# First layer of a four-layer network: gathers of the middle taps in three parts a round, finished tiles a round later

## The chip, the core and the metric

The kernel is written in Bass and Tile for one NeuronCore of a Trainium2 chip. The core has five engines that run side by side, each in its own program order: TensorE (PE, matrix products into PSUM), VectorE (DVE), ScalarE (ACT), GpSimd (POOL), and SyncE (SP), which only issues DMAs here. They wait for one another by semaphores. The metric is the device time of one execution in microseconds; smaller is better.

## The reference, cut to the first layer

The network has four layers over an input of 4 images, 128 channels, 64 x 64 places. Only the first is touched by the change: a group norm, then a deformable convolution with 8 groups and 9 taps, a product with `w_out`, a batch norm, and x * sigmoid(x), added to the input.

```python
val = xf @ w_value + b_value                     # xf: normed input, places x channels
om  = (xf @ w_off + b_off).reshape(N, P, G, OM)  # per place and group: 18 offsets, 9 masks
sy, sx = base_y + offset[..., 1], base_x + offset[..., 0]
...
for dy, dx, wgt in ((0, 0, (1 - ty) * (1 - tx)), (0, 1, (1 - ty) * tx),
                    (1, 0, ty * (1 - tx)), (1, 1, ty * tx)):
    acc = acc + gather(iy, ix) * (wgt * valid(iy, ix))[..., None]
out = (acc * mask[..., None]).sum(axis=3)
out = out.reshape(N, P, C) @ w_out + b_out
...
return out * jax.nn.sigmoid(out)                 # after the batch norm
```

The later layers (a convolution with a state-space scan, a cosine "attention" with a feed-forward part, tanh attention, and two expert mixtures) run after it, unchanged.

## The kernel before

**Two ways for a place.** Nearly all offsets are small. A place whose offsets stay within R = 1 is computed without any gather: a 5 x 5 window of values around it (W = 5) is multiplied with 25 weights per group. Places with a larger offset, up to R2 = 2, are "exceptions": each image may have up to 128 of them, one to a partition, and they are computed from a 7 x 7 window (W2 = 7) whose rows are gathered one by one from a table in DRAM.

**Tiles and rounds.** An image is 8 tiles (NQS = 8) of TG = 4 columns of 128 places. The loop at the end of the first layer runs over rounds r; round r does tile r of the 32 tiles of the 4 images (so rounds 0 to 7 are image 0, 8 to 15 image 1, and so on), and beside it

- projects a tile of the next image (`project`, `evict`: values to the table `tab`, offsets to `oms`) and ranks its exceptions (`flags`, `rank`, `collect`),
- makes the weights of tile r + 1 (`tents`, `weights`),
- takes one step of the generator `exceptions(n)` after each of the five parts k = 0 to 4 of the round,
- turns tile r - 1 (`cast`, then `turn`: four transposes and a copy into `aT`), and
- finishes tiles whose image has its exceptions ready.

In part k, PE adds the products of window column k into PSUM (`accumulate`, five 512-wide products with the identity), and DVE makes those of column k + 1 (`multiply`, tile `pr`, 128 x 2560). `multiply` also has SP load that column for the next tile (`move`, tile `v`). In part 4 the first product of the next round is made, ahead of the step of `exceptions`.

**The exceptions.** `exceptions(n)` starts in the second round of image n (r % 8 == 1). It makes the row numbers `idx`, and then for each of the seven columns s gathers seven sets of rows into `px` (seven indirect DMAs of POOL, one for each u) with two `px` buffers. The weights of the exceptions are worked out after the first gather. Then, for each s, column s + 1 is gathered and column s is multiplied with its weights on DVE and added into `total`. In the end PE folds `total` (`pe1`), multiplies with `w_out` (`pe2`), and ACT leaves the result in `tw` (`mended[n]`). Each `yield` ends a step. A gather has a `yield` inside it, after its fourth DMA, so its seven DMAs fall into steps of four and three, and the generator has 17 steps: the gathers lie in steps 1 to 14, the last product in step 15, `pe1` in 16, `pe2` in 17. Step 17 is taken in part 1 of the fourth round after the start's (r % 8 == 4).

**Finishing.** `spread` transposes the marks of the exceptions of a tile (`ohs`, made by DVE in part 0, into `oT`), and `finish`, one part later, multiplies the turned tile `aT` with `w_out` and adds the exceptions through `oT` and `tw`; ACT applies the batch norm and the last function, and POOL adds the result into X (`settle`). It needs `mended[n]`. The dictionary `ends` says in which round which tiles are finished; a finish starts in part 2, a second one follows in part 3 (or 4). `turned` holds the copies `aT` until then, in 4 buffers.

**What sets the order.** All engines' instructions in this loop go through `InOrder`, which keeps each engine in the program's order; only the DMAs of SP are free of it. A DVE product that waits for gathered rows therefore holds up everything behind it on DVE. PSUM tiles of `turn`, `spread`, `finish` and the exceptions share two buffers (tag `pt`).

In the profile nearly all instructions of this loop are put down to line 82, the helper that keeps the order, so they are told apart by the names of their tiles.

Of the kernel before, what the change touches and what calls it, by code (L numbers as in the profile page):

```python
# [8 lines left out]
F32 = mybir.dt.float32  # L9
# [7 lines left out]
P = 128  # L17
# [71 lines left out]
class Kernel:  # L89
# [33 lines left out]
    def layer0(self):  # L123
# [12 lines left out]
        TG = 4  # L136
# [6 lines left out]
        with ExitStack() as outer:  # L143
            fp = outer.enter_context(tc.tile_pool(name="d0x", bufs=1))
            over = fp.tile([1, 1], I32, name="over")
            with ExitStack() as ctx:
# [4 lines left out]
                qp = ctx.enter_context(tc.tile_pool(name="d0q", bufs=2))  # L151
# [7 lines left out]
                for n in range(NB):  # L159
                    for h in range(2):  # L160
                        s = slice(n * L + h * L // 2, n * L + (h + 1) * L // 2)
# [139 lines left out]
                def tents(om, m, r):  # L301

                    D = 2 * r + 1
                    o = om[:, 0:18 * m]
                    tent = wp.tile([P, D, 18 * m], F32, name=f"tent{r}", tag="tent")
                    ab = wp.tile([P, 18 * m], F32, name=f"ab{r}", tag="t0")
                    for d in range(-r, r + 1):
                        if abs(d) == r:
                            k = R2 + r - 1
                            nc.scalar.activation(tent[:, d + r, :], o, AF.Relu, bias=shift[:, k:k + 1],  # L310
                                                 scale=float(d // r))
                        else:
                            nc.scalar.activation(ab, o, AF.Abs, bias=shift[:, d + R2:d + R2 + 1])
                            nc.scalar.activation(tent[:, d + r, :], ab, AF.Relu, bias=self.ones[:, 0:1],
                                                 scale=-1.0)
                    return tent
# [131 lines left out]


                mended = {}  # L450

                def exceptions(n):
                    oc = wp.tile([P, NO + 1, G], F32, name="oc")
                    ocf = oc.rearrange("p j g -> p (j g)")
                    nc.scalar.copy(ocf, rare[n][:, 0:(NO + 1) * G])
                    idx = wp.tile([P, W2, W2], I32, name="idx")
                    nc.vector.tensor_scalar(idx, reach, oc[:, NO, 0:1], None, ALU.add)
                    flat = tabs[n].rearrange("x y c -> (x y) c")
                    wt = wp.tile([P, W2, W2, G], F32, name="wt2")

                    def gather(s):
                        px = qp.tile([P, W2, P], F32, name="px")
                        for u in range(W2):
                            nc.gpsimd.indirect_dma_start(
                                out=px[:, u, :], out_offset=None, in_=flat,
                                in_offset=bass.IndirectOffsetOnAxis(ap=idx[:, s, u:u + 1], axis=0))
                            if u == 3:
                                yield
                        return px

                    px = yield from gather(0)
                    yield "weights"
                    for _ in weights(ocf, tents(ocf, G, R2), wt, G, R2):
                        pass
                    total = wp.tile([P, W2, P], F32, name="total")
                    for s in range(W2):
                        after = (yield from gather(s + 1)) if s + 1 < W2 else None
                        dst = px if s else total
                        nc.vector.tensor_tensor(
                            dst.rearrange("p u (g c) -> p (u g) c", c=CG),  # L480
                            px.rearrange("p u (g c) -> p (u g) c", c=CG),
                            wt[:, s].rearrange("p u g -> p (u g)").unsqueeze(2).to_broadcast([P, W2 * G, CG]),
                            ALU.mult)
                        if s:
                            nc.vector.tensor_tensor(total, total, px, ALU.add)
                        px = after
                        yield
                    ps = pt.tile([P, TG * P], F32, name="pe1", tag="pt")
                    for u in range(W2):
                        nc.tensor.matmul(ps[:, 0:P], total[:, u, :], self.ident, start=(u == 0), stop=(u == W2 - 1))  # L490
                    eT = sm.tile([P, P], F32, name="eT", bufs=1)
                    nc.scalar.copy(eT, ps[:, 0:P])
                    yield
                    ps = pt.tile([P, TG * P], F32, name="pe2", tag="pt")
                    nc.tensor.matmul(ps[:, 0:P], eT, w_out, start=True, stop=True)
                    tw = sm.tile([P, P], F32, name="tw", bufs=2)
                    nc.scalar.copy(tw, ps[:, 0:P])
                    mended[n] = tw
# [51 lines left out]
                def turn(i, at_):  # L550
                    pT = pt.tile([P, TG * P], F32, name="pT", tag="pt")
                    for k in range(TG):
                        nc.tensor.transpose(pT[:, k * P:(k + 1) * P], at_[:, k * P:(k + 1) * P], self.ident)
                    aT = qp.tile([P, TG * P], F32, name="aT", bufs=4)
                    nc.scalar.copy(aT, pT)
                    turned[i] = aT

# [21 lines left out]
                LAST_R = NB * NQS  # L579
                ends = {}  # L580
                for n in range(NB):
                    for k, qs in ((4, (0, 1)), (5, (2, 3)), (6, (4,)), (7, (5,)), (8, (6, 7))):
                        ends.setdefault(n * NQS + k, []).extend(n * NQS + q for q in qs)
                extra, stat, tent, wgen = None, None, None, None
                order(0)
# [1 line left out]
                for r in range(-4, LAST_R + 1):  # L587
# [34 lines left out]
                    for k in range(W):  # L622
# [29 lines left out]
                        if k == 1:  # L652
                            if at_ is not None:
                                turn(r - 1, at_)
# [1841 lines left out]
```

## Time and profile before

| | us |
|---|---|
| Three timed runs | 5593.98, 5611.95, 5615.91 (median 5611.95) |
| The profiled execution, its own time | 5601.23 |
| Its span in the profile | 5599.5 |
| First `pr` product starts | 108.2 |
| Last tile is added into X | 1145 |

The span of the profile and the time of the same execution are 1.7 us apart, so sums made in the profile can be read as time. The first layer takes the first fifth of the span; the rest does not depend on the change except by starting earlier or later.

Busy time of the engines from the first `pr` product (108.2 us) to the last (1128.7 us), 1020.5 us in all:

| Engine | busy us |
|---|---|
| PE | 921.5 |
| DVE | 874.4 |
| POOL | 414.9 |
| ACT | 231.2 |

Averages over this stretch hide that the rounds differ. Rounds that hold gathers have POOL busy most of their length; other rounds have POOL nearly idle. Some rows for the instructions that the change moves:

| Instruction | count | duration, us |
|---|---|---|
| gather `px<-tab,idx` (POOL) | 196 | 0.94 to 3.56, median 1.17 |
| product `px<-px,wt` (DVE) | 24 | 1.09 |
| sum `total<-total,px` (DVE) | 24 | 1.09 |
| product `pr<-v,wt` (DVE) | 160 | 2.82 |
| copy `aT<-pT` (ACT) | 32 | 0.59 |

A gather's duration is what POOL spends on it; the rows arrive after it. A row of the timeline has the start, the duration, the engine, the source line, the operation, the tiles (out<-in), the shape, and in brackets the idle time of the engine before it with what ended it.

### The profile page before, as it was taken

To read this page: it belongs to the slowest core of one execution; us is meant where nothing else is said; L and a number is where in the kernel's file an instruction comes from. 1 tells how busy PE (TensorE), PEld (TensorE's weight loads), DVE (VectorE), ACT (ScalarE), POOL (GpSimd) and SP (SyncE) were. 2 spreads that over 40 slices of the span, in tenths; PEclk is the share of its full clock that TensorE was granted. 3 is DMA by queue.
4 is the path that set the end of the run, shared out by engine and by line. 5 is a ranking of instruction groups with operands and counts; after the bars stand their busy time and mean duration, and the time that the engine had idled before them with its cause. 6 is when DMAs were issued, how large, how long until landed. Compare 5 with 4: busy or idle time off the path is not lost. (4 is left out here: it accounts for less than half of the span.)

```text
span 5599.5 us, 62830 instructions
## 1 busy us (share of the span) xinstructions
PE 4991.9 (89%) x21718; PEld 2404.9 (43%) x21718; DVE 4016.3 (72%) x7854; ACT 3113.9 (56%) x3785; POOL 3073.1 (55%) x3027
## 2 busy tenths in 40 slices
PE   6898989879999859999887899989998998999887
PEld 3454444335656523333443344434433444344443
DVE  6888988758876578786698565666566666665796
ACT  1122222146655345555431689878978987889431
POOL 0525253314444324454399577666766776667597
PEclk8999999989988779999899899999999999999899
DMA  5545454400000020000000000000000000000001
GB/s 171 126 131 128 124 132 127 98 6 1 16 16 12 27 61 1 1 1 1 6 31 16 16 1 1 1 1 1 1 1 1 1 1 1 1 1 1 5 1 61
DMA packets 66743, 185.21 MB, mean 33 GB/s; under 512 B 13158, under 2 KB 16038, under 8 KB 64744
## 3 DMA queue, kind: packets, MB, share of 16 engines
q1 hardware_dynamic: 55792, 163.68, 9.9%
q0 software_dynamic: 6272, 12.86, 1.4%
q10 hardware_dynamic: 4344, 4.50, 0.3%
q8 instruction: 175, 2.87, 0.2%
q14 instruction: 160, 1.31, 0.1%
HBM read 131.63 MB, written 49.36 MB: 32 GB/s over the span
## 5 line engine op out<-in xcount | busy, mean ns | idle before, releaser
L82 POOL TENSOR_TENSOR r<-r 128x512 f32<-128x512 f32 (+1 forms) x1088 | 1349.0, 1241 | 661.9 <-DVE r L82 597.0
L82 DVE TENSOR_TENSOR r<-r,num 128x1024 f32<-128x1024 f32 (+1 forms) x1088 | 970.4, 927 | 564.3 <-PE num L82 514.1
L82 PE MATMUL D<-F,G 32*128 32x512 f32 (+3 forms) x4608 | 1218.8, 589 | 1.9 <-POOL G L82 1.0
L82 PE MATMUL num<-F,G 32*128 32x512 f32 (+3 forms) x4608 | 1084.5, 604 | 105.4 <-DVE r L82 101.6
L82 ACT ACTIVATE r<-r 128x2048 f32<-128x2048 f32 (+4 forms) x610 | 1018.3, 1679 | 49.2 <-POOL r L82 3.4
L82 ACT ACTIVATE r<-D 128x1536 f32<-128x1536 f32 (+1 forms) x544 | 764.2, 1405 | 206.1 <-PE D L82 174.2
L82 PE MATMUL acc<-pr,ident 128*128 128x512 f32 x1600 | 749.4, 619 | 79.4 <-DVE pr L82 79.4
L82 PEld LDWEIGHTS D<-F,G 32*128 32x128 f32 x4608 | 507.2, 189 | 327.4 <-issue 217.2
L82 PE MATMUL acc<-r,v 128*128 128x512 f32 (+3 forms) x1152 | 606.4, 614 | 3.1 <-DVE aT L82 3.1
L82 PEld LDWEIGHTS num<-F,G 32*128 32x128 f32 x4608 | 394.4, 187 | 410.9 <-DVE r L82 239.5
L1886 PE MATMUL pex<-w_expert_w,vT 128*128 128x512 f32 x1024 | 489.5, 618 | 78.9 <-DVE x L1889 78.8
L1896 POOL TENSOR_TENSOR x<-x 128x512 f32<-128x512 f32 (+2 forms) x576 | 472.6, 820 | 103.3 <-DVE x L1889 73.3
L82 PEld LDWEIGHTS acc<-pr,ident 128*128 128x128 f32 x1600 | 309.9, 198 | 439.4 <-issue 340.2
L82 DVE TENSOR_TENSOR pr<-v,wt 128x2560 f32<-128x2560 f32 x160 | 452.7, 2835 | 30.3 <-PE acc L82 24.6
L82 PE MATMUL pff<-hid,w_ffn_w2T 128*128 128x512 f32 x1024 | 468.4, 600 | 0.0
L82 POOL DMA_INDIRECT px<-tab,idx x196 | 330.7, 1687 | 231.5 <-DVE idx L82 159.8
L82 POOL TENSOR_TENSOR X<-X,sl 128x512 f32<-128x512 f32 x32 | 87.9, 2746 | 491.5 <-ACT sl L82 491.5
L1889 DVE TENSOR_TENSOR x<-pex,gate 128x1024 f32<-128x1024 f32 x256 | 309.1, 1213 | 62.8 <-POOL X L1897 51.1
L82 PEld LDWEIGHTS acc<-r,v 128*128 128x128 f32 x1152 | 176.7, 190 | 393.1 <-issue 263.9
L1886 PEld LDWEIGHTS pex<-w_expert_w,vT 128*128 128x128 f32 x1024 | 184.0, 193 | 329.0 <-DVE x L1889 176.9
L82 ACT ACTIVATE hid<-phh,cols 128x512 f32<-128x512 f32 x320 | 198.9, 685 | 224.2 <-PE phh L82 224.2
L82 POOL TENSOR_TENSOR Y<-y,tm 128x64 f32<-128x64 f32 x256 | 115.9, 473 | 331.1 <-DVE w L82 164.3
(563 smaller groups left out, 7379.4 us busy)
## 6 DMA issues: line engine op xcount, KB each, us to landing
v<-tab SPq DMA_DIRECT2D x320, 256.0 KB
oms<-omw SPq DMA_DIRECT2D x32, 432.0 KB
omr<-oms SPq DMA_DIRECT2D x32, 432.0 KB
X<-in_x_dram SPq DMA_DIRECT2D x8, 1024.0 KB
tab<-vb SPq DMA_DIRECT2D x64, 128.0 KB
o<-o SPq DMA_DIRECT2D x32, 256.0 KB
oin<-o SPq DMA_DIRECT2D x32, 256.0 KB
kept<-X SPq DMA_DIRECT2D x4, 2048.0 KB
```

Of the source, the lines that this page charges most:

```text
L82: return lambda *args, **kwargs: self.tc.keep_in_program_order(op(*args, **kwargs))
L1886: nc.tensor.matmul(pex[:, 4 * h:4 * h + 4, :], vT[:, k, :], ew[:, 512 * h:512 * (h + 1)], start=True, stop=True)
L1889: nc.vector.tensor_tensor(x, pex, gate[:, k, :].unsqueeze(2).to_broadcast([P, NE, P]), ALU.mult)
L1896: nc.gpsimd.tensor_tensor(x[:, 0:w, :], x[:, 0:w, :], x[:, w:2 * w, :], ALU.add)
```

## The change

Three edits. First, the gathers of columns s = 1 to 5 (`PACED`) have their inner `yield` after the third and after the fifth DMA, so that seven DMAs fall into steps of three, two and two; columns 0 and 6 keep four and three. The generator then has 22 steps: gathers in steps 1 to 19, the products of columns 0 to 6 in steps 5, 8, 11, 14, 17, 19 and 20, `pe1` in step 21, `pe2` in step 22. Step 22 is taken in part 1 of the round with r % 8 == 5. Second, the tiles of an image are finished two a round, in the fifth to the eighth round counted from the image's first as 0, instead of 2, 2, 1, 1, 2 in the fourth to the eighth. Third, `aT` has five buffers.

```diff
                 mended = {}
+                PACED = range(1, 6)
 
                 def exceptions(n):
...
                             nc.gpsimd.indirect_dma_start(
                                 out=px[:, u, :], out_offset=None, in_=flat,
                                 in_offset=bass.IndirectOffsetOnAxis(ap=idx[:, s, u:u + 1], axis=0))
-                            if u == 3:
+                            if u == 3 and s not in PACED or u in (2, 4) and s in PACED:
                                 yield
                         return px
...
-                    aT = qp.tile([P, TG * P], F32, name="aT", bufs=4)
+                    aT = qp.tile([P, TG * P], F32, name="aT", bufs=5)
                     nc.scalar.copy(aT, pT)
                     turned[i] = aT
...
-                    for k, qs in ((4, (0, 1)), (5, (2, 3)), (6, (4,)), (7, (5,)), (8, (6, 7))):
+                    for k, qs in ((5, (0, 1)), (6, (2, 3)), (7, (4, 5)), (8, (6, 7))):
                         ends.setdefault(n * NQS + k, []).extend(n * NQS + q for q in qs)
```

## The prediction

> **What bounds the kernel now.** I read the granted clock and DMA rows of the page first, to place the first layer (it ends near 1145 us of 5599.5), then cut it into its rounds. A round starts at every fifth `pr` product on DVE. Image 1 spans rounds 9 to 16; this is the table of busy time by stretch over them. Columns: stretch, length, busy time and instructions of PE, PEld, DVE, ACT, POOL, then granted clock, DMA share, GB/s.
>
> ```profile
> 402.80:436.50 33.70, 29.15 (x78) 14.41 (x77) 31.16 (x50) 13.04 (x32) 22.53 (x13) 0.92 0.51 128
> 436.50:468.50 32.00, 28.57 (x78) 13.97 (x77) 29.40 (x41) 5.86 (x14) 27.62 (x15) 0.98 0.58 142
> 468.50:516.10 47.60, 34.74 (x92) 17.78 (x90) 38.17 (x60) 8.47 (x20) 34.45 (x23) 0.86 0.54 132
> 516.10:548.60 32.50, 29.36 (x90) 15.20 (x91) 28.52 (x47) 5.32 (x11) 1.27 (x1) 0.95 0.38 108
> 548.60:579.10 30.50, 30.50 (x91) 15.72 (x90) 26.77 (x46) 8.38 (x19) 7.32 (x2) 1.00 0.43 114
> 579.10:609.10 30.00, 30.00 (x87) 15.33 (x86) 25.94 (x41) 10.70 (x23) 6.55 (x2) 1.00 0.46 126
> 609.10:637.50 28.40, 28.40 (x84) 14.60 (x83) 25.79 (x42) 7.11 (x16) 2.85 (x1) 1.00 0.48 134
> 637.50:666.20 28.70, 28.70 (x87) 14.93 (x86) 26.44 (x45) 4.74 (x12) 3.64 (x1) 1.00 0.48 131
> ```
>
> Two regimes. Rounds 13 to 16 have PE busy from end to end: PE sets the time. In rounds 9 to 12, where the 49 gathers run on POOL, PE is below its length and DVE is the busiest, with a hole of 9.4 us in round 11. The waits of the first 1100 us say who made the hole (total, times, longest):
>
> ```profile
> POOL px L82 <- issue: 55.2, 181, 0.3
> DVE px L82 <- DMA px<-tab,idx: 46.5, 14, 7.3
> ```
>
> POOL stands 0.3 us between gathers 181 times out of 196: it issues without pause. DVE waits 46.5 us for gathered rows, and 3.6 us more in image 2 (put down to issue). The POOL and DVE timelines at the hole of round 11:
>
> ```profile
> 467.90 0.94 POOL L82 DMA_INDIRECT px<-tab,idx  x1 [0.30 <-issue]
> 469.15 2.99 POOL L82 DMA_INDIRECT px<-tab,idx  x1 [0.30 <-issue]
> 472.45 0.94 POOL L82 DMA_INDIRECT px<-tab,idx  x1 [0.31 <-issue]
> ```
>
> ```profile
> 468.50 2.83 DVE L82 TENSOR_TENSOR pr<-v,wt 128x2560 f32<-128x2560 f32 x1
> 476.22 1.10 DVE L82 TENSOR_TENSOR px<-px,wt 128x896 f32<-128x896 f32 x1 [4.89 <-DMA px<-tab,idx]
> ```
>
> The seventh gather of its tile ends on POOL at 472.1 and the product starts at 476.2: about 4 us of landing. DVE stands in program order, so every later product, and PE behind it, stands too. Image 3 is worst, because its rounds hold less DVE work while POOL's stay the same:
>
> ```profile
> 981.60:1023.30 41.70, 30.46 (x64) 12.96 (x64) 26.83 (x23) 6.20 (x15) 35.00 (x23) 0.88 0.56 120
> ```
>
> Why: before, a gather of 7 takes two of the five steps of a round, so 17.5 gathers a round. Start to start they are 2.02 us apart (mean over the four trains), 35.4 us a round against 25 to 31 us of DVE work. The px waits per image, from the waits of each four-round stretch: 6.2, 5.2, 13.9, 24.8, together 50.1 us.
>
> **Part 1, the three-part gathers.** Tiles 1 to 5 take three steps, so a round holds 11.7 gathers in the middle. Nothing is added: 196 gathers, 28 products, the same DMAs; no SP transfer moves. Steps per image go from 17 to 22. The products (1.09 + 1.09 us) shift: by the generator, the stretches of rounds 9 to 12 held products 0; 1, 2; 3, 4, 5; 6, and will hold none; 0, 1; 2, 3; 4, 5, with 6 at the start of round 13.
>
> What sets the new pace is the gather spacing under a busier DVE. Laying the POOL timeline against DVE's: the 35 intervals with DVE under half busy average 1.25 us, the 24 at 50 to 90% average 2.41, the 133 at 90% and more 2.16. So DVE work slows descriptor making already. A rule speaks against the change here: the Trainium skill, "SBUF — State Buffer", has a box on DVE blocking gathers of the POOL queue, and its section on the wrong bandwidth-pool intuition prices one at 0.62 us alone and 3.1 us beside a two-port DVE copy. At 3.1, a train is 49 x 3.1 = 152 us, longer than the four rounds before, and the change would lose. At 2.16 it is 106 us. I take the row: two thirds of today's intervals are already under a full DVE. The three steps between two products are some 18 us against 7 x 2.16 = 15.1, so POOL keeps up.
>
> One tight place stays: tile 6 can start only when product 4 frees its px buffer (two exist), and its product comes three steps later, as before. 7 x 2.16 + 3.5 landing is 18.6 against about 17.5 of DVE work: 1.1 us of wait per image; below nothing is excluded (a wait cannot be negative), above is 4.2 (spacing 2.6).
>
> DVE sums of the four rounds: today 127.1, 127.3, 121.4, 102.6 for images 0 to 3. Off come product 6 (2.17) and the marks of two tiles (eight `ohs`, 1.65): 3.8. Idle that stays is the length less DVE busy less the px waits, less the 3.7 and 3.6 us that DVE waited for PE in round 4 of images 0 and 1: 8.5, 9.7, 4.9, 8.7. To it I add 2.0 for the fourth round, now ruled by DVE and showing the waits of rounds 9 and 10 (1.2 for the rank and 0.8 for the accumulation), and the 1.1.
> - Image 0: 127.1 - 3.8 + 8.5 + 3.1 = 134.9, before 145.5: -10.6
> - Image 1: 127.3 - 3.8 + 9.7 + 3.1 = 136.3, before 145.8: -9.5
> - Image 2: 121.4 - 3.8 + 4.9 + 3.1 = 125.6, before 140.2: -14.6
> - Image 3: the same sum gives 110.6, but POOL is late: its train starts 12.0 us into the stretch, and 12.0 + 49 x 2.1 + 3.5, less the 2.8 of the `pr` ahead of product 6, is 115.6 (2.1 because DVE will be some 87% busy, between the train's 2.01 today and 2.16). Before 136.1: -20.5
>
> Sum -55.2 us. Below: 2.02 spacing gives image 3 back 4 us. Above: 2.41 costs 4 in image 2 and 15 in image 3.
>
> **Part 2, the finishes a round later.** Tiles 0 to 7 of an image are finished 2, 2, 2, 2 in rounds 5 to 8 where it was 2, 2, 1, 1, 2 in rounds 4 to 8. One finish on PE, from its timeline in round 13:
>
> ```profile
> 564.20 0.60 PE L82 MATMUL poh<-ident,ohs 128*128 128x128 f32 x4
> ...
> 569.50 1.02 PE L82 MATMUL pO<-aT,w_w_out 128*128 128x512 f32 x2
> 570.36 1.02 PE L82 MATMUL pO<-oT,tw 128*128 128x512 f32 x2
> 571.22 0.60 PE L82 MATMUL poh<-ident,ohs 128*128 128x128 f32 x4
> ```
>
> Start to start: 0.43 + 0.86 + 0.86 = 2.15 us. The turned tile's transposes start at 563.76, 594.24, 622.56, 650.89: 30.48 with two finishes, 28.32 with one, the same 2.16. These two finishes leave a round where DVE will rule and enter rounds 6 and 7, ruled by PE: +4.3. The sixteen short `pe` matmuls also move from round 4 to round 5, 0.108 each by the transposes' spacing: +1.7. So +6.0 per image, +24.1 in all; no cover hides it, since PE is 100% busy there (image 3's rounds 29 to 31 show DVE waiting 4.9 us a round for the accumulation, the same bound). PE may enter round 13 up to 2 us less behind, by the gap between `pr` and its accumulation today (1.8 to 2.2): I leave this as range.
>
> **Part 3, five buffers.** 2 KB a partition and no instruction. Tile 4's copy in round 5 precedes finish 0; the next reuse follows a finish by a round: no wait. Finishes wait for `tw` as now, one round later. On POOL the adds into X (1.3 to 3.9 us) come after the last gather in both orders; nobody queues behind them.
>
> A second rule: the Trainium skill, "TensorE: Matmul & The Clock Gate", on clock oscillation, says that idle gaps over some 3.4 us halve PE's clock. The row agrees in kind (PE's longest wait for `pr` is 4.5 us, clock 0.86 in round 11), and by the rule closing gaps would give round 11 up to 0.14 x 47.6 = 6.7 us of PE time. By the row that is worth nothing: round 10 has 0.98 and is still 32.0 us, with DVE at 29.4. I take 0.
>
> **Sum:** -55.2 + 24.1 = -31 us. Against the profiled run's own 5601.2 us: 5570. Against the median of 5612: 5581. The four known times average 5607, and I forecast 5575 between them. About 0.5% (28 us) is what a measurement can tell here, so the forecast stands close to that line.
>
> **Rivals.**
> - Gathers slow down to 2.4 us as DVE closes up. For it: the 2.41 of the middle class. Against: the fullest class has 2.16. It costs 19 us: -12, some 5595, within 0.5%.
> - POOL becomes the bound everywhere (slower). Stretches become train start (9.3, 11.3, 11.4, 12.0 us) + 49 s + 0.7. They lose all gain over the +24 at s = 2.53; at 3.1 the four are 87 us longer than today, and with +24 the time is about 5718. For it: the skill's price. Against: no class of intervals reaches 2.53.
> - The px waits are landing time, not rate, and stay. For it: products start 3 to 5 us after the last gather in nearly every tile. Against: tiles 4 and 5 of images 0 and 1, where round 3's statistics give POOL time, are used 12 us after, without a wait. Then 50 us stay, finishes and product moved: 5601 - 15 + 24 = 5610: no change.
>
> **Chances.** Forecast 0.62 (own range 5560 to 5592), slowed gathers 0.20, landing 0.09, POOL bound 0.09. Of the forecast's 0.62 some 0.08 falls short of 28 us; of the slowed gathers 0.03 is beyond it. Faster 0.57, same 0.34, slower 0.09. The range of 5555 to 5600 takes in the spacing's ends and the slowed gathers.
>
> **What will show it.** px waits under 10 us in all; rounds 9 to 12 near 32.5, 31, 41, 31.5; rounds 13 to 16 near 32, 30.5, 30.5, 30.5, PE full; image 3's four rounds near 115; gather spacing 2.1 to 2.2. Wrong if the spacing passes 2.4, if px waits stay over 25 us, or if rounds 13 to 16 grow by much more than 6 us together.

## The result, and the profile after

The changed kernel takes 5582.3 us (median of 17 runs, 5549.8 to 5592.8), the kernel before 5602.1 (median of 17 runs timed beside it). The ratio is 0.9962, with a 95% interval of 0.9951 to 0.9972: faster by 0.38%, some 21 us, where 31 had been forecast. In the profiled executions the last tile of the first layer is added into X at 1124.7 us where it was 1145.6, so the gain lies in the first layer.

Busy time by stretch, rounds 9 to 16 of the changed kernel (columns as before: stretch, length, PE, PEld, DVE, ACT, POOL, clock, DMA share, GB/s):

```profile
400.10:433.00 32.90, 28.35 (x77) 14.14 (x76) 30.35 (x48) 13.06 (x32) 21.92 (x13) 0.92 0.50 125
433.00:463.20 30.20, 28.84 (x79) 14.33 (x78) 28.25 (x41) 5.86 (x14) 23.12 (x13) 0.97 0.58 151
463.20:505.80 42.60, 32.58 (x92) 17.14 (x90) 36.04 (x59) 8.46 (x20) 24.30 (x17) 0.88 0.53 135
505.80:537.80 32.00, 27.77 (x69) 13.12 (x70) 29.01 (x41) 4.92 (x11) 16.41 (x9) 0.89 0.49 120
537.80:571.60 33.80, 29.64 (x97) 15.75 (x96) 28.62 (x48) 6.37 (x15) 6.54 (x2) 1.00 0.42 112
571.60:602.10 30.50, 30.50 (x92) 15.72 (x91) 26.77 (x46) 8.38 (x19) 7.32 (x2) 1.00 0.45 127
602.10:632.60 30.50, 30.50 (x92) 15.74 (x91) 26.77 (x46) 8.38 (x19) 7.32 (x2) 1.00 0.45 125
632.60:663.00 30.40, 30.40 (x91) 15.69 (x90) 26.67 (x45) 8.28 (x19) 7.31 (x2) 1.00 0.44 124
```

The gathers no longer fill POOL in rounds 10 and 11, and DVE's idle time in round 11 is smaller (6.6 us of 42.6, before 9.4 of 47.6). PE is busy from end to end in rounds 14 to 16, at 30.5 us each. Round 13 is the odd one: 33.8 us, with neither PE nor DVE busy throughout. The waits of the changed kernel's first layer (total, times, longest), of POOL and of DVE:

```profile
POOL px L82 <- DVE total L82: 73.8, 12, 13.5
...
DVE px L82 <- DMA px<-tab,idx: 29.2, 8, 6.1
```

POOL now stands 73.8 us for a `px` buffer that DVE frees: in images 0 to 2 it is ahead, not behind. DVE still waits 29.2 us for rows, 8 times. Cut by stretch, these waits (px waits below) are 4.2, 4.2 and 4.1 us in rounds 5, 13 and 21, and 16.7 in image 3. The table adds the rounds up (from the starts of every fifth `pr` product):

| rounds | before, us | after, us | difference | forecast |
|---|---|---|---|---|
| 1 to 4 | 145.5 | 136.5 | -9.0 | -10.6 |
| 9 to 12 | 145.8 | 137.7 | -8.1 | -9.5 |
| 17 to 20 | 140.2 | 123.0 | -17.2 | -14.6 |
| 25 to 28 | 136.1 | 117.7 | -18.4 | -20.5 |
| 5 to 8, 13 to 16, 21 to 24, 29 to 31 | 421.4 | 452.5 | +31.1 | +24.1 |

### The profile page after: what moved, and what is told of

Its sections match the earlier page's. It is cut to its first block, busy times and chain, and to the rows that moved or that the text cites. A ratio compares the mean times of both kernels' runs of the same rounds, so it can differ in the third digit from the quotient of the medians.

```text
span 5583.2 us, 62833 instructions
## 1 busy us (share of the span) xinstructions
PE 4990.0 (89%) x21718; PEld 2405.5 (43%) x21718; DVE 4020.2 (72%) x7854; ACT 3113.5 (56%) x3785; POOL 3102.9 (56%) x3027
## 5 line engine op out<-in xcount | busy, mean ns | idle before, releaser
L82 PE MATMUL acc<-pr,ident 128*128 128x512 f32 x1600 | 736.2, 609 | 63.2 <-DVE pr L82 63.0
L82 POOL DMA_INDIRECT px<-tab,idx x196 | 359.4, 1834 | 295.1 <-DVE idx L82 158.5
## 6 DMA issues: line engine op xcount, KB each, us to landing
X<-in_x_dram SPq DMA_DIRECT2D x8, 1024.0 KB, 10.6
```

The lines of the kernel that those rows point to most:

```text
L82: return lambda *args, **kwargs: self.tc.keep_in_program_order(op(*args, **kwargs))
```

## The experiments

A ratio is the time of a version divided by that of the kernel before, timed beside it; its 95% interval stands in brackets. Versions without a ratio were run once, and are read from their profiles.

**The finishes alone.** The kernel before with the second and third edit only.

```diff
-for k, qs in ((4, (0, 1)), (5, (2, 3)), (6, (4,)), (7, (5,)), (8, (6, 7))):
+for k, qs in ((5, (0, 1)), (6, (2, 3)), (7, (4, 5)), (8, (6, 7))):
```

> The kernel before, with only the finishes moved a round later and five aT buffers; its gathers stay in four and three. My theory: the later place alone buys nothing. Round 12, freed of two finishes and still with the px wait before it, falls from 32.5 us to 29 to 30.5; rounds 14 and 15 rise from 30.0 and 28.3 to 30.5 each; px waits stay near 46 us in all. Net about +1 us an image, a ratio of 1.000 to 1.002. Rival: the later place is itself a gain, since PE had been the bound in round 12: then the ratio is 0.998 or less.

The ratio was 0.9997 (0.9987 to 1.0008). Round 12 fell to 29.4, rounds 14 and 15 came to 30.5; round 13, where I had named no change, fell to 28.8. The gathers were as late as ever:

```profile
DVE px L82 <- DMA px<-tab,idx: 47.5, 15, 6.1
```

This is the wait row of the 1000 us or so of the first layer's rounds. The last tile was added into X at 1147.1 us, where it was 1145.6. So the later place alone gains nothing and costs nothing clear of the noise, and the 21 us belong to the new spacing of the gathers that is put on top of it.

**A third px buffer, after and before.** The `px` ring gets `bufs=3`. To make room, tiles that only the set-up uses are moved into it, four in the changed kernel and one in the kernel before.

```diff
-px = qp.tile([P, W2, P], F32, name="px")
+px = qp.tile([P, W2, P], F32, name="px", bufs=3)
```

In the changed kernel:

> The changed kernel with a third px buffer (its room is found by letting set-up tiles use the ring). Theory: product 6 waits 4.2 us in rounds 5, 13 and 21 because its gather may start only when product 4 frees a buffer; with three buffers these waits go, rounds 5, 13 and 21 fall from 34 us to about 32.2, and image 3, where POOL issues without pause anyway, stays at 117 to 119 us in rounds 25 to 28 with its px waits. Together -5 to -6 us. Rival: the waits are landing time or POOL's pace; then they stay at 3 us or more.

In the kernel before:

> The kernel before with a third px buffer. If POOL's pace was the cause of the px waits before the change, a buffer more changes little: px waits stay at 40 us or more, the four rounds of each image within 3 us of 145.5, 145.9, 140.2 and 136.1. If the two buffers held the gathers back, px waits fall below 15 us and the four rounds by 5, 5, 14 and 20 us.

In the changed kernel the first layer's last add came at 1113.9 us, 10.8 earlier. Rounds 5, 13 and 21 took 30.8 us each, not 34, and waited for no rows; image 3's rounds 25 to 28 stayed at 118.3. The gain was twice what I had expected. These rounds fell below the 32.2 us of PE work that I had summed for them, since PE enters them less far behind DVE: its first accumulation of round 13 starts 0.05 us after its product, where it was 2.14 us in the kernel before. Another 2.2 us came in rounds 1 to 4. The mechanism stands in the changed kernel's own timelines. First POOL, then DVE, then PE, around the start of round 13:

```profile
525.58 3.28 POOL L82 DMA_INDIRECT px<-tab,idx  x1 [13.40 <-DVE total L82]
...
538.06 3.40 POOL L82 DMA_INDIRECT px<-tab,idx  x1 [0.30 <-issue]
```

```profile
537.83 2.83 DVE L82 TENSOR_TENSOR pr<-v,wt 128x2560 f32<-128x2560 f32 x1
544.87 1.09 DVE L82 TENSOR_TENSOR px<-px,wt 128x896 f32<-128x896 f32 x1 [4.22 <-DMA px<-tab,idx]
```

```profile
540.71 4.56 PE L82 MATMUL acc<-pr,ident 128*128 128x512 f32 x10 [1.64 <-DVE pr L82]
...
547.14 1.83 PE L82 MATMUL pe<-ident,total 128*128 128x128 f32 x14 [0.96 <-DVE total L82]
549.88 4.56 PE L82 MATMUL acc<-pr,ident 128*128 128x512 f32 x10 [0.91 <-DVE pr L82]
```

POOL had idled 13.4 us for the buffer; the last tile's seven gathers then took 15.9 us and landed 3.4 later, DVE stood 4.2 us, and PE stood behind DVE at each of the three rows shown. The first of its waits, 1.64 us, is there with the third buffer too (1.63); the other two are not.

In the kernel before, the buffer did nothing. Of DVE's px waits, 42.5 us are put down to DMA and 9.4 to issue, 51.9 beside 50.1 without it, and POOL issued as densely:

```profile
DVE px L82 <- DMA px<-tab,idx: 42.5, 13, 6.2
...
DVE px L82 <- issue: 9.4, 2, 5.1
...
POOL px L82 <- issue: 57.0, 187, 0.3
```

Before the change it was POOL's pace; after it, for three images, the buffer of the last tile.

The ratio of the changed kernel with the third buffer was 0.9917 (0.9895 to 0.9938), too much for 11 us, so it was timed again.

> The same kernel as in the run with a third px buffer, timed longer. There the first layer was 11 us shorter than in the changed kernel, but the second layer, which the edit does not touch, was 18 us shorter as well (872 against 890 us), with less time at half clock (229 against 283 us). If that is chance of the execution, the second layer's time here lies anywhere from 872 to 900 us and the ratio moves to 0.993 to 0.996 (the changed kernel's 0.9962 less 11 us); if it belongs to this kernel, the second layer stays at 870 to 875 us and the ratio at 0.990 to 0.993. The first layer ends within 1 us of the first time in both.

The ratio was now 0.9939 (0.9919 to 0.9958), and the first layer ended at 1113.9 again. But the second layer was short here too, at 873.6 us. The ratio speaks for chance, the profile for the kernel; the two intervals overlap, and which it is stays open. The third buffer alone does not bring it: a version below that has it too, the one with moved finishes, took 895.0 us there. What differs in that layer is shown in the last section.

**No gathers.** The products read one tile of zeros.

```diff
-nc.gpsimd.indirect_dma_start(out=px[:, u, :], ...)
-px = qp.tile([P, W2, P], F32, name="px")
+px = spare                      # zeroed once
```

> The changed kernel with no gather at all: the products of the exceptions read one tile of zeros, so the exceptions' values are left out; all products, waits of DVE and finishes stay. It shows what the gathers still cost. Theory: rounds 9 to 12 fall little, from 137.7 to 135 to 137; round 13 from 33.8 to about 32.2; rounds 25 to 28 from 117.7 to 103 to 108 us, round 29 from 32.1 to 29; some 25 us in all, most of it image 3. Rival: image 3's four rounds are held by PE or by something else than POOL and stay over 113.

Rounds 9 to 12 took 137.7 us, round 13 30.8, rounds 25 to 28 107.9 and round 29 26.8. The first layer's last add came at 1097.5, 27 us ahead of the changed kernel. So in rounds 9 to 12 nothing of the gathers is left to gain. What is left is image 3, with 10 us in rounds 25 to 28 and 5 in round 29, the 3 us each of rounds 5, 13 and 21, and 2.6 us in rounds 1 to 4.

**Why image 3 stays slow.** Its 49 gathers took 111.9 us from first to last, 2.28 us each, where I had counted 2.1. One gather, and what DVE did meanwhile:

```profile
959.21 6.36 POOL L82 DMA_INDIRECT px<-tab,idx  x1 [0.31 <-issue]
```

```profile
959.20 5.54 DVE L82 TENSOR_TENSOR pr<-v,wt 128x2560 f32<-128x2560 f32 x2
```

The gather starts with two large products that follow each other, and ends 0.83 us after both. It is no single case. Laid against DVE's timeline, 71 of the changed kernel's 196 gathers have a `pr` product end inside them: they take 3.05 us in the mean, and each of them ends 0.81 to 1.04 us after that product. The 95 gathers that meet no such product take 1.18 us in the mean and never more than 1.76; the other 30 end within the first 0.95 us of one. (In the kernel before it is 54 gathers of 3.03 us with the same 0.81 to 1.04, and 118 of 1.16.) So I cut these products in two.

```diff
-nc.vector.tensor_tensor(pr4, v, wt4, ALU.mult)
+for u0, u1 in ((0, 3), (3, W)) if 25 <= i < 30 else ((0, W),):
+    nc.vector.tensor_tensor(pr4[:, u0:u1], v[:, u0:u1], wt4[:, u0:u1], ALU.mult)
```

> The changed kernel with the large product pr of the tiles 25 to 29 (image 3's gather rounds) made by two instructions of three and two window columns instead of one of five. Theory: a gather that meets a DVE product waits for its end, so image 3's gathers come 2.28 us apart (49 in 112 us) although DVE is only some 85% busy; halves let a waiting gather in earlier. Then the train of image 3 falls from 112 to 98 to 106 us and rounds 25 to 29 from 149.8 by 4 to 10 us. Rival: the slow pace is the gathers' own, or that of DMA; then the train stays at 109 us or more and the rounds rise by the two more instructions a product.

The train took 98.1 us, rounds 25 to 28 took 106.3 and rounds 29 to 31 79.4 (before the cut 117.7 and 81.6). Rounds 25 to 29 fell by 13.2 us, more than the 4 to 10 expected, and the first layer ended 15.2 us earlier. A pair of halves takes 2.89 us where one product took 2.82. DVE's waits from 900 to 1105 us:

```profile
DVE pr L82 <- PE acc L82: 16.9, 9, 3.1
DVE px L82 <- issue: 4.8, 1, 4.8
```

Of the 16.7 us of px waits in image 3 one of 4.8 us is left, in round 29. Its row names no DMA, but the product starts 3.9 us after the last gather ended on POOL, as in the waits for rows above. For the rest it is PE that DVE waits for now.

The cut does a second thing, which the theory did not hold: PE starts on the first half while DVE makes the second. DVE and PE of the later version with cut and third buffer:

```profile
993.17 2.89 DVE L82 TENSOR_TENSOR pr<-v,wt 128x1536 f32<-128x1536 f32 x2
```

```profile
994.97 5.53 PE L82 MATMUL acc<-pr,ident 128*128 128x512 f32 x9 [2.76 <-DVE pr L82]
```

PE starts 1.1 us before the halves end at 996.06; with whole products it never starts before their end. So not all the time that the cut gains comes from POOL; the length of the train and the px waits tell what does.

**The same cut in the kernel before.** If the pace was the cause there, the cut must help without any of the three edits.

```diff
+for u0, u1 in ((0, 3), (3, W)) if 1 <= i % NQS < 5 else ((0, W),):
```

> The kernel before (gathers in four and three, finishes as they were), with the product pr split in two in the gather rounds of all images (tiles 1 to 4, 9 to 12, 17 to 20, 25 to 28). If POOL's pace beside DVE was the cause of the px waits, a faster pace alone takes a good part of them away without any new spacing: gather trains of 98 us fall to 80 to 92, px waits from 50 us to 15 to 35, the first layer ends 10 to 30 us earlier than before. If the spacing of the steps was the cause, px waits stay over 40 us.

The trains fell to 93.4, 91.3, 84.3 and 85.8 us, and the last add came at 1104.5, 41 us earlier than before and 20 earlier than with the change. The first train stayed a little over the 80 to 92 that I had expected, and the gain was over my 10 to 30. The px waits are 15.9 us, of which 13.5 lie in image 3:

```profile
DVE px L82 <- DMA px<-tab,idx: 9.1, 3, 4.6
DVE px L82 <- issue: 6.8, 2, 6.0
```

The cut keeps the early finishes, so the later rounds cost what they did (117.6 us), while rounds 1 to 4 fall to 138.4, 9 to 12 to 138.7, 17 to 20 to 127.4 and 25 to 28 to 124.3. The px waits fell from 50.1 to 15.9 us with spacing and buffers as they were. That shows the pace of the gathers beside DVE as the cause of the old stall, and spacing as the dearer of two cures. These 34 us are the greater part of the 41; how much of the other 7 is PE's earlier start was not measured apart.

**Finishes into the next image's gather rounds.** On top of the third buffer:

```diff
+late = ((5, (0, 1)), (6, (2,)), (7, (3,)), (8, (4,)), (9, (5,)), (10, (6,)), (11, (7,)))
+full = ((5, (0, 1)), (6, (2, 3)), (7, (4, 5)), (8, (6, 7)))
+for k, qs in late if n + 1 < NB else full:
...
+eng = nc.vector if (NB - 2) * NQS + 5 <= i < (NB - 1) * NQS else nc.gpsimd
+eng.tensor_tensor(xs, xs, tile_order(sl), ALU.add)
```

> The changed kernel with the third px buffer, and of images 0 to 2 three finishes moved on into the next image's gather rounds: two in round 5, one each in rounds 6 to 11 (those of image 2 that fall into rounds 25 to 27 are added into X by DVE instead of POOL). Theory: a finish costs 2.16 us where PE sets the time and only its marks (0.8 us of DVE) where DVE does, and next to nothing in image 3's rounds, where POOL sets the time. Rounds 14 to 16 fall from 30.5 to 28.3 each, rounds 9 to 11 and 17 to 19 rise by 0.8 to 1.2 each, rounds 25 to 28 stay within 2 us of 118. First layer 11 to 15 us shorter than with the third px buffer alone. Rival: a finish costs the same wherever it lies, and POOL's adds between the gathers delay them; then the first layer is not shorter by more than 4 us.

A miss, and the rival's outcome. Rounds 15 and 16 fell to 28.3 as expected and round 14 only to 30.0; rounds 9 to 12 rose from 137.0 to 145.2 and rounds 17 to 20 from 122.9 to 128.5, while rounds 25 to 28 fell from 118.3 to 115.3. The first layer ended 1.3 us earlier, and the ratio was 0.9937 (0.9917 to 0.9957), no better than without. A finish was not just 0.8 us of marks. DVE's longest wait in round 9, PE behind it, and ACT ahead of it:

```profile
DVE tent L82 <- ACT tent L82: 3.9, 1, 3.9
```

```profile
425.07 6.00 PE L82 MATMUL acc<-pr,ident 128*128 128x512 f32 x10 [7.09 <-DVE pr L82]
```

```profile
413.21 0.78 ACT L82 ACTIVATE sl<-pO,bbi,bsc 128x512 f32<-128x512 f32 x1 [4.74 <-PE pO L82]
413.89 0.40 ACT L82 ACTIVATE tent<-oc,shift 128x144 f32<-128x144 f32 x1
```

ACT works in program order. The finish's last function waited 4.7 us for PE there, and the weights of the exceptions (`tent`) stood behind it on ACT; DVE stood for them, and PE for DVE. Of the 8.2 us, 3.8 are more work on DVE and 4.4 more idle time; how much of them and of the 5.6 us the other finishes brought, I have not taken apart.

**The best of both.** First the third buffer and the cut together.

> The changed kernel with both edits that helped alone: the third px buffer (rounds 5, 13, 21 fall by 3 us each) and the split products of tiles 25 to 29 (rounds 25 to 31 shorter by 13.6 us). They act on different rounds, so they should add: the first layer ends 10.8 + 15.2 = 26 us earlier than in the changed kernel, near 1099 us, beside 1097.5 with no gathers at all. Ratio to the kernel before 0.989 to 0.993, with the second layer's 872 to 900 us as the part that no edit here sets. Rival: with the products split, the third buffer is no longer needed or DVE's additional instructions eat the gain: then the first layer ends at 1105 us or later.

They added: the last add came at 1098.2, beside 1097.5 with no gathers. The two are not alike in their parts: rounds 25 to 28 took 105.3 us, 2.6 less than with no gathers, and DVE's waits for PE in them 4.8 us, 2.7 less. With no gather left to wait for in the other version, the cut must gain these 2.6 us by something else than POOL's pace, and PE's earlier start is what the profile shows. The ratio is 0.9914 (0.9900 to 0.9928). Then, with the third buffer kept, the change's spacing and later finishes were left to image 3 alone, and the cut was made in the gather rounds of every image (and in round 29).

```diff
+PACED = range(1, 6) if n == NB - 1 else ()
...
+early = ((4, (0, 1)), (5, (2, 3)), (6, (4,)), (7, (5,)), (8, (6, 7)))
+late = ((5, (0, 1)), (6, (2, 3)), (7, (4, 5)), (8, (6, 7)))
+for k, qs in early if n + 1 < NB else late:
```

> A version put together from what the runs showed: split products in the gather rounds of every image, a third px buffer, gathers in four and three and finishes as in the kernel before for images 0 to 2, and the changed spacing and finishes for image 3 alone. Theory: images 0 to 2 keep the 117.6, 117.6 and 111.3 us of their later rounds and the 138.4, 138.7, 127.4 us of the split alone; image 3 keeps 105.3 and 77.5 us. The first layer's last add into X then comes near 1090 us, 8 us ahead of the version with third buffer and split products, and the ratio to the kernel before is 0.987 to 0.991. Rival: without the later finishes, images 0 to 2 give back what image 3 gains: then not ahead of 1096 us.

The last add came at 1087.3 us, 37 earlier than with the change, and the time was 5539.6 us (median of 6 runs): a ratio of 0.9888 (0.9869 to 0.9906). It is the lowest of all, and its interval still overlaps that of the version before it; the rounds tell the two apart. Rounds 9 to 12 took 138.8 us, 13 to 16 117.6, 25 to 28 106.5.

## Why the prediction was right, and where it was short

**What bounds the kernel: right.** Two regimes, POOL's pace as the cause of the stall, DVE in program order as what carries it on. The third buffer in the kernel before changed nothing, and the cut there took two thirds of the px waits away: the first excludes the buffers as the cause, the second shows the pace. One reading was too wide: the 9.4 us of round 11 are all of DVE's idle time. The wait for rows is 4.9 of them, and 3.8 are waits for PE's statistics (`bn`, `gmv`, `rstd`), which no spacing of gathers takes away.

**Part 1, rounds 1 to 28: right in kind, 2.5 us short in sum** (-52.7 against -55.2). Rounds 17 to 20 gained more than forecast, since DVE stood only 0.8 to 2.6 us a round there and the waits that I had added for the fourth round did not come. Images 0 and 1 gained 1.5 us less each: DVE's waits for ACT's `rk` and PE's `rstd`, 3.4 and 3.1 us together before, became 7.3 and 7.9, a rise of more than the 2.0 that I had added.

**The wait for tile 6: the term that failed.** I had 1.1 us an image, from 15.1 us of gathers, 3.5 of landing and 17.5 of DVE work in between. The wait was 4.2 us. Gathers and landing were 19.3 us as measured, near the sum; DVE's three steps were shorter, from the buffer's release at 525.3 to the end of the `pr` product at 540.7, that is 15.4. That the wait is just the upper end I had named is chance: I had reached 4.2 with gathers 2.6 us apart. I had also put the wait into the four gather rounds, where DVE has it to itself. It fell into round 13, where PE is the bound, and cost 3.0 us an image there: with the third buffer, rounds 13 to 16 took 122.2 us, without it 125.2.

**Part 2, finishes at 2.16 us each in PE's rounds: right.** Rounds 14 to 16 are 30.5 us, to the tenth. With the wait gone, the later rounds cost 122.2 - 117.6 = 4.6 us an image where I had 6.0. The 1.4 between them fits the lag of PE that I had left as range ("up to 2 us less behind"); at the start of round 13 it is 2.1 us less, as told at the third buffer. So the +31.1 against +24.1 is, in each of images 0 to 2, 3.0 for the wait less 1.4 for the lag, some 5 us together, and 2.1 in image 3. There rounds 29 to 31 cost 8.1 us more than before, with a wait for rows of 6.1 in round 29, and the third buffer changed nothing: it was POOL's pace. In sum the rounds became 21.6 us shorter, where 31.1 had been forecast.

**The gather spacing: mis-sized in image 3.** I took 2.1; it was 2.28, because that image's rounds consist of large products in close order, each of which holds a gather. Beside a full DVE the 2.2 us held in the first three images (2.19 over the 109 intervals at 90% and more in which POOL did not wait for a buffer); with image 3 it is 2.25 over 140. The Trainium skill ("SBUF — State Buffer", section on the wrong bandwidth-pool intuition) says that a DMA of the POOL queue beside a DVE copy is blocked until the copy ends. The trace and the cut show such a wait here, beside products that are no copies. The page's 3.1 us is near what a gather takes that a product holds, 3.05 us in the mean; it was not reached over a train, because 95 gathers of 196 met no such product. That is why taking the measured row instead of the page's price was right.

**The rivals.** "Gathers slow down" came half true, in image 3 only. "POOL becomes the bound everywhere" was not seen, since POOL waits 73.8 us for buffers. "The waits are landing time" falls with the cut in the kernel before: the products that still wait there start 3.3 to 4.8 us after their last gather, so the landing is no shorter, and 34 of the 50 us went. Two of the marks I had set tripped: px waits of 29 us, over the 25, and rounds 13 to 16 at +7.6. The time of 5582 lies in the range, between the forecast of 5575 and the 5595 of slowed gathers; the gain of 0.38% fell short of the 0.5% to which I had given 0.57.

## What to carry to other kernels

When a queue of gathers runs beside a busy VectorE, look at the longest VectorE instruction as well as at the number of gathers: cutting it in two cost 0.07 us a product and bought more than new spacing, in the main because gathers got in sooner, and in part because TensorE could start on the first half. A wait that is moved is priced in the round where it lands: here 4.2 us of VectorE's waiting cost 3.0 us in a round for which only TensorE's work had been summed. And work moved from a full engine into a round with room still takes its place in every queue that it uses; read the order of all of them, ACT's too.

## What the runs showed of the hardware

The second layer, which no edit touches, took from 872 to 902 us in the profiled executions, and was longer the lower its granted clock was (0.88 at 872 us, 0.84 at 902). Busy time by stretch of this layer in the kernel before, after, after with a third buffer (first run), and before with a third buffer:

```profile
1169.80:2059.90 890.10, 760.18 (x3856) 476.88 (x3854) 626.72 (x1859) 471.66 (x854) 323.51 (x542) 0.86 0.07 21
```

```profile
1148.90:2039.10 890.20, 764.25 (x3851) 481.44 (x3849) 628.00 (x1859) 471.48 (x854) 322.82 (x542) 0.85 0.06 21
```

```profile
1137.80:2009.90 872.10, 742.25 (x3856) 465.78 (x3854) 625.90 (x1859) 471.82 (x853) 323.82 (x542) 0.88 0.07 21
```

```profile
1172.00:2074.40 902.40, 773.37 (x3855) 486.28 (x3853) 628.16 (x1859) 471.97 (x854) 323.22 (x542) 0.84 0.06 21
```

DVE's work is the same in all four within 2.3 us; PE's differs by 31 us, and the clock from 0.84 to 0.88. The clock's records show full or half speed alone, and in these stretches 257, 270, 215 and 287 us at half (an expectation above has 283 and 229 for the second and third, which is too much). A change of 20 us in the first layer is therefore not read from one execution's total, but from the rounds: in the two profiles of the same kernel with the third buffer each round repeats within 0.1 us, but for one that differs by 0.33. What sets the share of half clock in the second layer, I have not found out.
